# Cross-attention weights of a transformer stack, turned by 32x32 blocks and two transfers instead of transposes on TensorE

## The chip, the cores and the metric

The kernel runs on one core of a Trainium2 chip. The metric is the device time of one execution in microseconds. Before the change it is 2530.57 us, the median of three runs (2528.28 to 2533.17).

The engines are named as in the profile: PE (TensorE, matrix products; PEld is its loading of stationary operands), DVE (VectorE), ACT (ScalarE), POOL (GpSimd) and SP (SyncE, which issues the transfers). PSUM is the memory that PE writes its results to.

## The reference

Four attention blocks follow each other on a tensor x of 8 batches x 256 rows x 128 features, with a context of 8 x 64 rows x 64 features and a mask of 8 x 256 x 256. The third block is a stack of six layers, and the change touches only that one. Each layer does

```
tn = norm(t);  t = mha(tn, tn,  skv, sq, sow, sob, mask)     + t     # self-attention
tn = norm(t);  t = mha(ctx, tn, ckv, cq, cow, cob, ctx_mask) + t     # cross-attention
tn = norm(t);  t = t + (relu(tn @ w1 + b1) @ w2 + b2)
```

with 16 heads of 64, so `ckv` is 64 x 2048 (keys and values), `cq` 128 x 1024 and `cow` 1024 x 128. In `mha` the scores of a head are q k^T / 8, then a softmax, the sum of values, and the product with the output weights.

In cross-attention the keys come from a context that never changes. So for each head the product of query and key weights (64 x 128) and that of value and output weights can be made once a layer and used for all eight batches. This is called folding below.

## The kernel before

All arithmetic is in float32. Activations `t` stay on the chip; weights of a layer are loaded ahead into buffers of which there is one each. Work is written as small steps, each given a tick and a phase with `at(tick, phase, fn)`. At the end (L1195 to L1211) the steps are issued in the order of tick and phase, and each instruction of PE, DVE, ACT and POOL is chained to the one before it on its engine. So the order on these four engines is the written one: an engine that waits holds back everything behind it. SP is not chained; its transfers are put in an order when the program is built.

A layer starts at tick T0. Batch b has its self-attention at T0 + 4b to T0 + 4b + 6 (`plan_sa`, L818), overlapping with its neighbours, cross-attention begins at T_ca = T0 + 32 (`plan_ca`, L1018), and the feed-forward part at T_ca + 16. "Tick 20" below means T0 + 20. In the profiled second layer the scores of tick 20 start on PE at 714.12 us, those of tick 21 at 721.38, 22 at 728.83, 23 at 736.35, 24 at 744.11, 26 at 758.83, 27 at 767.37, 28 at 775.78, 29 at 779.57 and 30 at 789.04.

In a self-attention tick PE does two score tiles (L866), then by turns the values (L921), the output product `out_proj` (L939), and the projections of a later batch: k and q (L829) and v (L848). DVE adds the mask and takes the row minimum of each score quarter (L880), ACT does the exponentials (L885), DVE the reciprocal of the sums (L893), POOL the division (L895), and DVE turns the result by 32x32 blocks (L905, `turn`) for the values. DVE and ACT each empty one of the two tiles of the values ("o copy", L284 and L286), and ACT empties the projections. `add_out` (L945) adds the output product to `t` on DVE in phase 8.2.

PSUM holds four tiles of two banks (`two_banks`, L45), used in turn: a new tile waits until the tile four allocations back is emptied. The "o" buffers on the chip (`big("o")`) are also four in turn; the values of self-attention, the hidden layer of the feed-forward part and the transposed cross-attention weights use them.

The weights of cross-attention are prepared by `plan_ca_weights(l, T)` with T = T_ca - 6, at the end of self-attention. In ticks 26 and 27 `turned` makes eight 128x128 transposes on PE each (L983), of `ckv` (whose keys lie on partitions 0 to 63 and values on 64 to 127) and of `cq`, into one PSUM tile; ACT copies it into an "o" buffer (L989, L991), the queries' one with the scale 1/8. In ticks 28 and 29 `folded` makes AT and WVO with 32 matmuls each (L1001) into two PSUM tiles, which ACT copies (L1007). `keys_both` (L1022) uses AT in tick 30 first.

Each batch's mask is loaded by SP (`load_mask`, L242) into one of two buffers, two ticks ahead of its scores in the written order.

Of the kernel before, what the change touches and what calls it, by code (L numbers as in the profile page):

```python
# [8 lines left out]
F32 = mybir.dt.float32  # L9
# [7 lines left out]
P = 128  # L17
B, S, D = 8, 256, 128
M, DM = 64, 64
NL, H, HD, FF = 6, 16, 64, 512  # L20
HC = H * HD // P
# [6 lines left out]
def tile_xattn_stack(ctx: ExitStack, tc: tile.TileContext, io, out: bass.AP):  # L28
    nc = tc.nc
# [11 lines left out]
    def uniq(base):  # L41
        counter[0] += 1
        return f"{base}_{counter[0]}"

    def two_banks(base):  # L45
        return psum.tile([P, 1024], F32, tag="ps", name=uniq(base))
# [10 lines left out]
    def big(tag, bufs=4, shape=(P, 1024), dtype=F32):  # L57

        return heap.tile(list(shape), dtype, tag=tag, name=uniq(tag), bufs=bufs)

    def sb(shape, tag, bufs=2, pool=None):
        return (pool or act).tile(shape, F32, tag=tag, name=uniq(tag), bufs=bufs)
# [46 lines left out]
    ident = const.tile([P, P], F32, tag="ident", name="ident")  # L109
# [10 lines left out]
    for i in range(4):  # L120
# [52 lines left out]
        out=hmask, in_=hmask, compare_op=ALU.is_ge, fill=0.0, base=0,  # L173
# [3 lines left out]
        out=hmask, in_=hmask, compare_op=ALU.is_ge, fill=0.0, base=7,  # L177
# [3 lines left out]
    for r in range(2):  # L181
        rows = slice(64 * r, 64 * r + 64)
# [10 lines left out]
    W = {}  # L193
# [44 lines left out]
    dram = ctx.enter_context(tc.tile_pool(name="dram", bufs=1, space=bass.MemoryType.DRAM))  # L238
# [40 lines left out]
    def at(tick, phase, fn):  # L279
        plan.setdefault(tick, []).append((phase, fn))  # L280
# [692 lines left out]
    def plan_ca_weights(l, T):  # L973


        st = {}
        W["fold", l] = st

        def turned(name, w, scale):
            def fn():  # L980
                ps = two_banks("tp")
                for c in range(HC):
                    nc.tensor.transpose(  # L983
                        ps[:, c * P : (c + 1) * P], w()[:, c * P : (c + 1) * P], ident
                    )
                st[name] = big("o", shape=(P, HC, P))
                flat = st[name].rearrange("p c x -> p (c x)")
                if scale is None:
                    nc.scalar.copy(flat, ps)  # L989
                else:  # L990
                    nc.scalar.mul(flat, ps, scale)  # L991
            return fn

        def folded(name, cols, w):
            def fn():
                tiles = [two_banks("mm").rearrange("p (c d) -> p c d", c=HC) for _ in range(2)]
                res = sb([P, HC, D], name, 1, heap)
                for c in range(HC):
                    for r in range(2):
                        rows = slice(r * HD, (r + 1) * HD)  # L1000
                        nc.tensor.matmul(  # L1001
                            tiles[r][rows, c, :], lhsT=st["kvT"][rows, c, cols],
                            rhs=w()[rows, c, :], start=True, stop=True,
                        )
                for r in range(2):
                    rows = slice(r * HD, (r + 1) * HD)
                    nc.scalar.copy(res[rows], tiles[r][rows])  # L1007
                st[name] = res
            return fn

        at(T, 3.6, turned("kvT", lambda: W["ca", l][0], None))
        at(T + 1, 3.6, turned("WqT", lambda: W["ca", l][1], HD ** -0.5))
        at(T + 2, 3.6, folded("AT", slice(0, DM), lambda: st["WqT"]))
        at(T + 3, 3.6, folded("WVO", slice(DM, 2 * DM), lambda: W["ca", l][2]))

    keys_of = {}

# [154 lines left out]
    for l in range(NL):  # L1172
        T_ca = T0 + 4 * B
        T_ff = T_ca + 2 * B
        for b in range(B):
            plan_sa(l, b, T0 + 4 * b)
        plan_ca_weights(l, T_ca - 6)
        for b in range(B):
            plan_ca(l, b, T_ca + 2 * b)
            plan_ff(l, b, T_ff + b)  # L1180
        if l > 0:
            at(T0, -1, lambda l=l: load_ff(l))
        if l + 1 < NL:
            at(T_ca + 4, -1, lambda l=l: load_sa(l + 1))
            at(T_ff + 1, -1, lambda l=l: load_ca(l + 1))
        T0 = T_ff + B
# [14 lines left out]
    for tick in sorted(plan):  # L1201
        for _, fn in sorted(plan[tick], key=lambda item: item[0]):
            traced = nc.cur_bb.bb.instructions
            start = len(traced)
# [64 lines left out]
```

## Time and profile before

| what | us | share of the span |
|---|---|---|
| median of the runs | 2530.57 | |
| the profiled execution | 2528.09 | |
| its span, first to last instruction | 2526.4 | |
| PE busy | 2393.0 | 95% |
| DVE busy | 1822.0 | 72% |
| ACT busy | 1735.1 | 69% |
| POOL busy | 1443.0 | 57% |
| sixteen transposes of a layer, busy on PE, six layers (L983) | 13.2 | |
| their two copies on ACT, six layers (L989, L991) | 12.2 | |
| 32x32 turns of 128x512 on DVE, 768 of them (L905) | 519.9, 697 ns each | |
| division on POOL, 128x256, 1,536 of them (L895) | 702.5, 478 ns each | |

The mean granted clock of TensorE is 0.975 of full speed. A line of a timeline has the start in us, the length in us (of all instructions in it when several are merged, x8 for eight), the engine, the line of the kernel, the operation, what it writes and reads, and in brackets how long the engine sat idle before it and what ended that. A line of the chain of work in order of time has start, length, engine, what was written, line and number. Busy times of matmuls overlap each other, so the spacing of starts tells what a group takes of the queue.

### The profile page before, as it was taken

How to read it: one execution, taken by the hardware profiler on the slowest of the kernel's cores; microseconds unless marked ns; L12 is line 12 of the kernel's file. 1: busy time of each engine (PE TensorE's matmuls, PEld its weight loads, DVE VectorE, ACT ScalarE, POOL GpSimd, SP SyncE). 2: the span in 40 equal slices, each digit the busy share in tenths (PEclk: the TensorE clock that was granted, in tenths of full speed). 3: DMA queues.
4: the chain of work that ended last, by engine and by line, in shares of the span. 5: the costliest groups of instructions: out<-in, count | busy, mean ns of one | idle time of the engine just before them, and what ended most of it. 6: DMA issues, size and time to landing. Idle time of an engine off the chain costs nothing.

```text
span 2526.4 us, 100196 instructions
## 1 busy us (share of the span) xinstructions
PE 2393.0 (95%) x42507; PEld 1765.0 (70%) x42507; DVE 1822.0 (72%) x5976; ACT 1735.1 (69%) x4537; POOL 1443.0 (57%) x2477
## 2 busy tenths in 40 slices
PE   6899999999999999999989999989999989999996
PEld 3566777776777776777776777776777776777774
DVE  3677887748887747887747887747887756888764
ACT  3467777657777657777657777657778657778651
POOL 2655556845556844555854555854555763555763
PEclk8999999999999999999999999999999999999996
DMA  5000012000002000002000102000012000000000
GB/s 161 11 2 20 19 35 64 2 8 24 20 28 65 8 7 24 20 20 70 12 2 21 28 20 70 12 2 20 20 28 70 12 2 20 20 20 12 3 1 17
DMA packets 94770, 64.31 MB, mean 25 GB/s; under 512 B 7729, under 2 KB 90353, under 8 KB 94322
## 3 DMA queue, kind: packets, MB, share of 16 engines
q1 hardware_dynamic: 93874, 57.64, 8.3%
q8 instruction: 334, 5.47, 0.9%
q14 instruction: 114, 0.93, 0.1%
q10 hardware_dynamic: 448, 0.26, 0.0%
HBM read 55.78 MB, written 2.10 MB: 23 GB/s over the span
## 4 chain that ended last, share of the span: by engine, by line
PE 69%; POOL 13%; DVE 8%; ACT 7%; issue 3%; DMA 0%; POOLq 0%; DVEq 0%; SPq 0%; ACTq 0%
PE mm L921 14%; PE mm L829 13%; PE sc L866 12%; PE mm L939 7%; PE mm L848 7%; POOL e L360 6%; PE mm L1071 3%; DVE m L359 3%; PE mm L1088 3%; POOL e L372 3%; ACT e L357 2%; PE mm L388 2%; ACT e L885 2%; PE sc L341 1%; POOL rstd L784 1%
## 5 line engine op out<-in xcount | busy, mean ns | idle before, releaser
L895 POOL TENSOR_SCALAR e<-e,rs 128x256 f32<-128x256 f32 x1536 | 702.5, 478 | 690.8 <-DVE rs L893 682.2
L885 ACT ACTIVATE e<-e,mn 128x256 f32<-128x256 f32 x1536 | 758.3, 495 | 131.0 <-DVE mn L880 130.2
L880 DVE CUSTOM_DVE_ANT_0 e<-sc,nm 128x256 f32<-128x256 f32 x1536 | 542.8, 419 | 122.5 <-PE sc L866 122.3
L905 DVE STREAM_TRANSPOSE eTc<-e 128x512 f32<-128x512 f32 x768 | 519.9, 697 | 66.2 <-POOL e L895 64.6
L921 PE MATMUL mm<-eTc,v 32*64 32x256 f32 x12288 | 381.2, 386 | 18.5 <-ACT AT L1007 8.1
L866 PE MATMUL sc<-k,q 64*32 64x256 f32 x12288 | 378.9, 380 | 5.9 <-DVE mn L880 4.2
L921 PEld LDWEIGHTS mm<-eTc,v 32*64 32x64 f32 x12288 | 284.1, 134 | 112.5 <-issue 27.7
L866 PEld LDWEIGHTS sc<-k,q 64*32 64x32 f32 x12288 | 220.2, 106 | 125.3 <-issue 45.8
L360 POOL TENSOR_TENSOR e<-e,m 128x1024 f32<-128x1024 f32 x112 | 213.1, 1903 | 148.6 <-DVE m L359 141.9
L885 ACT ACTIVATION_READ_ACCUMULATOR e<-e,mn 128x1 f32 x1536 | 286.7, 187 | 0.0
L359 DVE TENSOR_REDUCE m<-sc 128x16 f32<-128x1024 f32 x112 | 137.2, 1225 | 179.4 <-ACT e L357 179.4
L388 PE MATMUL mm<-v,k 128*128 128x128 f32 x1792 | 235.5, 287 | 5.9 <-DVE k L380 5.4
L388 PEld LDWEIGHTS mm<-v,k 128*128 128x128 f32 x1792 | 219.1, 200 | 27.4 <-issue 12.1
L341 PE MATMUL sc<-q,tT 128*32 128x256 f32 x3072 | 217.1, 382 | 0.0
L372 POOL TENSOR_TENSOR e<-e,r 128x1024 f32<-128x1024 f32 x112 | 213.2, 1904 | 0.7 <-DVE r L371 0.7
L366 ACT ACTIVATE e<-e 128x1024 f32<-128x1024 f32 x112 | 119.0, 1062 | 115.8 <-POOL e L360 115.8
L829 PE MATMUL mm<-tT,w_sk 128*128 128x256 f32 x768 | 189.6, 390 | 0.0
L286 ACT COPY v<-mm 128x1024 f32<-128x1024 f32 x96 | 97.2, 1012 | 133.1 <-PE mm L848 133.1
L939 PEld LDWEIGHTS mm<-w_sow,o 128*128 128x128 f32 x1536 | 175.1, 192 | 17.7 <-issue 14.4
L848 PE MATMUL mm<-w_sv,tT 128*32 128x256 f32 x3072 | 185.7, 382 | 0.0
L939 PE MATMUL mm<-w_sow,o 128*128 128x128 f32 x1536 | 183.6, 278 | 1.5 <-ACT WVO L1007 1.5
L829 PE MATMUL mm<-tT,w_sq 128*128 128x256 f32 x768 | 173.6, 379 | 0.0
(210 smaller groups left out, 3521.9 us busy)
## 6 DMA issues: line engine op xcount, KB each, us to landing
nm<-mask_d SPq DMA_DIRECT2D x192, 128.0 KB, 3.0
w_sk<-in_L_sa_kv_dram SPq DMA_DIRECT2D x6, 512.0 KB, 9.4
w_sv<-in_L_sa_kv_dram SPq DMA_DIRECT2D x24, 128.0 KB, 2.4
w_sq<-in_L_sa_q_dram SPq DMA_DIRECT2D x6, 512.0 KB, 3.5
w_sow<-in_L_sa_ow_dram SPq DMA_DIRECT2D x6, 512.0 KB, 4.0
w_ckv<-in_L_ca_kv_dram SPq DMA_DIRECT2D x12, 256.0 KB, 4.2
w_cq<-in_L_ca_q_dram SPq DMA_DIRECT2D x6, 512.0 KB, 4.6
w_cow<-in_L_ca_ow_dram SPq DMA_DIRECT2D x6, 512.0 KB, 4.0
```

The source lines that it names most:

```text
L360: nc.gpsimd.tensor_tensor(e, e, m.unsqueeze(2).to_broadcast([P, 16, M]), ALU.subtract)
L372: nc.gpsimd.tensor_tensor(tl["e"], tl["e"], r.unsqueeze(2).to_broadcast([P, 16, M]), ALU.mult)
L388: nc.tensor.matmul(ps[:, :D], lhsT=eT[:, s].rearrange("p q x -> p (q x)"), rhs=vw[:, r, k, g, :], start=(s == 0), stop=(s == 7),)
L829: nc.tensor.matmul(ps[:, i * S : (i + 1) * S], lhsT=w[:, c * P : (c + 1) * P], rhs=st["tT"], start=True, stop=True,)
L848: nc.tensor.matmul(ps[32 * a : 32 * a + 32, i, :], lhsT=st["tT"][:, kb * 32 : (kb + 1) * 32], rhs=sv[:, a].rearrange("p g x -> p (g x)"), ...
L866: nc.tensor.matmul(sc[32 * a : 32 * a + 32, r, j, :], lhsT=st["q"][g][rows, a, qb * 32 : (qb + 1) * 32], rhs=st["k"][g][rows, a, :], start ...
L880: nc.vector.tensor_tensor_reduce(e[:, i, :], sc4[:, i, :], st["nm"][:, 2 * jj + i % 2, :], -1.0, 3.0 * BIG, ALU.add, ALU.min, mn[:, i : i ...
L885: nc.scalar.activation(e[:, i, :], e[:, i, :], AF.Exp, scale=-1.0, bias=mn[:, i : i + 1], accum_out=rs[:, i : i + 1],)
L895: nc.gpsimd.tensor_scalar(e[:, i, :], e[:, i, :], rs[:, i : i + 1], 1.0, ALU.mult, ALU.mult)
L905: nc.vector.transpose(eT[:, r, :, 2 * jj : 2 * jj + 2, :], e[:, 2 * r : 2 * r + 2, :].rearrange("p j (k x) -> p k j x", x=32),)
L921: nc.tensor.matmul(ops[a // 2][r * HD : (r + 1) * HD, a % 2, :S], lhsT=st["v"][kb // 4][rows, kb % 4, (2 * g + r) * HD : (2 * g + r + 1) * ...
L939: nc.tensor.matmul(st["ps"][:, j * D : (j + 1) * D], lhsT=st["oT"][c // 4][:, c % 4, j * P : (j + 1) * P], rhs=sow[:, c, :], start=(c == 0 ...
```

## The change

Both weights are now transposed without PE. `turned(i)`, i = 0 for `ckv` and 1 for `cq`, in ticks 20 and 21 at phase 8.7, turns a whole 128x1024 weight tile by 32x32 blocks in one DVE instruction into an "o" buffer z, and stores z with four transfers of 128 KB into a buffer in device memory. `fetched(i)`, in ticks 22 and 23 at phase -0.5, loads it back with one transfer of 512 KB over the weight tile itself, with the blocks' positions exchanged, so that after it the tile holds the transposed weights in runs of 32 elements. `regrouped`, in tick 27 at phase 8.05, copies the key and value weights on POOL into another order in an "o" buffer, so that 64 columns lie together as the stationary operand of `folded`. The query weights are read by `folded` as they lie, as a moving operand of four runs of 32. The scale 1/8 moves to the copies of AT on ACT. `folded` stays in ticks 28 and 29.

```diff
-        def turned(name, w, scale):
-            def fn():
-                ps = two_banks("tp")
-                for c in range(HC):
-                    nc.tensor.transpose(
-                        ps[:, c * P : (c + 1) * P], w()[:, c * P : (c + 1) * P], ident
-                    )
-                st[name] = big("o", shape=(P, HC, P))
-                flat = st[name].rearrange("p c x -> p (c x)")
-                if scale is None:
-                    nc.scalar.copy(flat, ps)
-                else:
-                    nc.scalar.mul(flat, ps, scale)
-            return fn
-
-        def folded(name, cols, w):
+        def turned(i):
+
+
+            w = W["ca", l][i]
+            z = big("o", shape=(P, 4, HC, 32))
+            nc.vector.transpose(z, w.rearrange("p (c j x) -> p j c x", j=4, x=32))
+            zd = dram.tile([4, 32, 4, HC * 32], F32, tag="wd", name=uniq("wd"), bufs=2)
+            for j in range(4):
+                nc.sync.dma_start(
+                    out=zd[j].rearrange("b i x -> i b x"),
+                    in_=z[:, j].rearrange("p c x -> p (c x)"),
+                )
+            W["cab", l, i] = zd
+
+        def fetched(i):
+            w = W["ca", l][i]
+            nc.sync.dma_start(out=w, in_=W.pop(("cab", l, i)).rearrange("j b i x -> (j b) (i x)"))
+            st[i] = w.rearrange("p (i c x) -> p i c x", i=4, x=32)
+
+        def regrouped():
+
+            st["kvT"] = big("o", shape=(P, HC, 4, 32))
+            nc.gpsimd.tensor_copy(st["kvT"].rearrange("p c i x -> p i c x"), st[0])
+
+        def folded(name, part, w, scale=None):
...
-                            tiles[r][rows, c, :], lhsT=st["kvT"][rows, c, cols],
-                            rhs=w()[rows, c, :], start=True, stop=True,
+                            tiles[r][rows, c, :],
+                            lhsT=st["kvT"][rows, c, 2 * part : 2 * part + 2, :].rearrange(
+                                "p i x -> p (i x)"
+                            ),
+                            rhs=w(c)[rows], start=True, stop=True,
...
-                    nc.scalar.copy(res[rows], tiles[r][rows])
+                    if scale is None:
+                        nc.scalar.copy(res[rows], tiles[r][rows])
+                    else:
+                        nc.scalar.mul(res[rows], tiles[r][rows], scale)
...
-        at(T, 3.6, turned("kvT", lambda: W["ca", l][0], None))
-        at(T + 1, 3.6, turned("WqT", lambda: W["ca", l][1], HD ** -0.5))
-        at(T + 2, 3.6, folded("AT", slice(0, DM), lambda: st["WqT"]))
-        at(T + 3, 3.6, folded("WVO", slice(DM, 2 * DM), lambda: W["ca", l][2]))
+        for i in range(2):
+            at(T - 6 + i, 8.7, lambda i=i: turned(i))
+            at(T - 4 + i, -0.5, lambda i=i: fetched(i))
+        at(T + 1, 8.05, regrouped)
+        at(T + 2, 3.6, folded("AT", 0, lambda c: st[1][:, :, c, :], HD ** -0.5))
+        at(T + 3, 3.6, folded("WVO", 1, lambda c: W["ca", l][2][:, c, :]))
```

## The prediction

> **What bounds the kernel now.** I read the page's busy shares and chain first, then the chain of work in order of time around the touched steps, then each engine's timeline there. Times are those of the second of the six layers; in all six the touched ticks show the same 1.02 us steps and the same DVE and ACT waits, to 0.1 us but for instruction-issue gaps. "Tick n" counts from the layer's T0.
>
> Busy shares, and the shares of the chain by engine:
>
> ```profile
> PE 2393.0 (95%) x42507; PEld 1765.0 (70%) x42507; DVE 1822.0 (72%) x5976; ACT 1735.1 (69%) x4537; POOL 1443.0 (57%) x2477
> PE 69%; POOL 13%; DVE 8%; ACT 7%; issue 3%; DMA 0%; POOLq 0%; DVEq 0%; SPq 0%; ACTq 0%
> ```
>
> TensorE is the bound over most of the span, and DMA is on no part of the chain. The chain through ticks 26 to 28 (start, length, what):
>
> ```profile
> 766.42 1.02 PE tp L983 x8
> 767.44 1.89 PE sc L866 x64
> ...
> 774.83 1.02 PE tp L983 x8
> 775.85 1.11 PE sc L866 x32
> ...
> 781.20 1.85 POOL e L895 x4
> ```
>
> Both removed steps lie on the chain, 1.02 us each. After the scores of tick 28 the chain leaves TensorE for DVE, POOL and ACT. PE's timeline there, idle time in brackets:
>
> ```profile
> 777.67 1.96 PE L1001 MATMUL mm<-o,o 64*64 64x128 f32 x32
> 779.57 1.96 PE L866 MATMUL sc<-k,q 64*32 64x256 f32 x64
> 782.50 0.66 PE L921 MATMUL mm<-eTc,v 32*64 32x256 f32 x8 [0.98 <-ACT AT L1007]
> 783.53 3.68 PE L921 MATMUL mm<-eTc,v 32*64 32x256 f32 x120 [0.37 <-ACT AT L1007]
> ```
>
> So after the AT fold (L1001) PE runs ahead and waits for ACT to empty its two PSUM tiles. DVE's timeline where the new turns go:
>
> ```profile
> 721.40 0.71 DVE L905 STREAM_TRANSPOSE eTc<-e 128x512 f32<-128x512 f32 x1 [0.19 <-POOL e L895]
> 722.58 0.42 DVE L880 CUSTOM_DVE_ANT_0 e<-sc,nm 128x256 f32<-128x256 f32 x1 [0.47 <-PE sc L866]
> ...
> 728.67 0.71 DVE L905 STREAM_TRANSPOSE eTc<-e 128x512 f32<-128x512 f32 x1 [0.20 <-POOL e L895]
> 730.03 0.42 DVE L880 CUSTOM_DVE_ANT_0 e<-sc,nm 128x256 f32<-128x256 f32 x1 [0.66 <-PE sc L866]
> ...
> 745.31 0.42 DVE L880 CUSTOM_DVE_ANT_0 e<-sc,nm 128x256 f32<-128x256 f32 x1 [0.67 <-PE sc L866]
> ```
>
> DVE has about half a microsecond free at the end of ticks 20 and 21, less than one turn. Last, POOL in tick 27 and ACT in tick 28:
>
> ```profile
> 772.79 3.65 POOL L895 TENSOR_SCALAR e<-e,rs 128x256 f32<-128x256 f32 x8 [4.89 <-DVE rs L893]
> ```
>
> ```profile
> 781.47 2.02 ACT L1007 COPY AT<-mm 64x1024 f32<-64x1024 f32 x2
> ```
>
> [...] eight in a row take only 1.02 us of the queue, 128 ns each; I use the spacing. [...] The trace's two 128x512 turns issue in 1.22 us (718.08 to 719.30)[...]. [...] Here POOL's one-input L895 takes 3.65 us for eight of 256, so 1.8 us per 1,024. [...] the 128 KB mask loads here land in 3.0 us.
>
> **The change, part by part.**
>
> *Removed from PE:* 2 steps x 1.02 us x 6 layers = 12.24 us. Is this really recovered? In ticks 26 and 27, DVE stood idle 1.44 and 1.62 us before the next scores, ACT 0.61 and 0.60, POOL 4.89 and 4.76, so all can follow PE 1.02 us earlier per step. The PSUM rotation gets shorter by one tile per tick; the tile that then comes four allocations back is freed in time (add_out ends at 767.14, the values of tick 27 would want it at 768.24; the v copy ends near 767.5). The two ACT copies (1.01 and 1.02 us) go too, worth nothing: ACT waits on both sides of them.
>
> *Added to DVE:* one turn of 128x1024 in each of ticks 20 and 21. Price: 2 x 0.61 = 1.22 us of queue; [...] upper end two rows of 697 ns, 1.39. No row of this size exists, but L905 and L380 read or write equally scattered runs of 32. Behind it in DVE's order is L880, which starts ACT's exponentials, then POOL's division. Tick 20: DVE is free at about 722.04, the turn ends at 723.26, L880 wanted 722.58: 0.68 late. That lateness goes round through ACT and POOL to the last turns of tick 21 (728.67), so the second turn starts near 729.99 and ends near 731.2, against 730.03: 1.17 late. Ticks 22 and 23 have no free time on DVE outside this loop (it is busy 7.65 of 7.76 us in tick 23), so 1.17 stays. Who waits? The values of tick 23 want the PSUM tile that add_out frees: 737.15 + 1.17 = 738.32 against 738.24. The scores of tick 24 want the tile that the o copy frees: 743.21 + 1.17 + 0.04 = 744.42 against 744.11. PE thus loses about 0.3 us per layer ([...] 0.6 with 1.39), and then DVE's idle 0.67 and the following gaps absorb the rest: 6 x 0.3 = 1.8 us.
>
> *Added to POOL:* the copy `regrouped` behind the eight divisions of tick 27. These start 1.02 earlier, at 771.77, and end at 775.42. With 1.8 us the copy ends at 777.22 [...]. But the AT fold, which reads kvT, would like to start at 777.67 - 2.04 = 775.63. So a new wait of about 1.63 us appears on PE, between the scores of tick 28 and the fold. It is nearly free: the fold then ends at 779.2, just before ACT gets to copy it (781.47 - 2.04 = 779.43). The scores of tick 29 end at 781.05, where the values could have begun at 780.46, and of these 0.59 us the 0.37 us second wait takes most: 8 matmuls end at 781.7 against 781.49. PE is about 0.2 late, and the next wait for ACT (0.24 us at 791.61) takes that. So the cost is 0 up to a copy of about 1.87 us, and each microsecond above costs one per layer. A copy of half that price gains nothing more, since ACT's chain then decides. POOL's own next work (781.20 - 2.04 = 779.16) waits for nothing. I take 1.8 us and 0.
>
> *The fold's operands:* the rhs of AT is now four runs of 32 instead of 128 in a row, the weights stay 64 in a row. The trace has no such rhs; L303 reads runs of 128 from a strided tile at 386 ns, like the contiguous L921. I take 0[...]. Scaling on the AT copy instead: 0 (1,015 against 1,002 ns for 128x1024).
>
> *Added to SP:* per layer 8 stores of 128 KB and 2 loads of 512 KB. Stores leave by about 724 and 732, loads by about 728 and 737, landing in 3.5 to 9.4 us as the weight loads do. The first need is POOL's at 775: over 25 us of cover. Behind them in SP's queue are mask loads; in before one is issued at 710.65 and the next near 740.6, wanted at about 745 and 775, so neither is pressed. [...] *The o buffers:* z0 and z1 stand between the oT tiles; the tile four back has passed its out_proj each time (tick 22.3 for the one wanted at 23.3), and z0 is stored long before tick 25. 0.
>
> Sum: -12.24 + 1.8 + 0 = -10.4 us. The profiled span of 2526.4 becomes 2516.0. That execution took 2528.09 us, 1.69 over its span and 2.5 under the median; from the median 2530.57 it makes 2520.2.
>
> **The rivals.** *A, DVE's lateness takes more:* a turn at 1.39 us or beyond, or lateness that reaches the q and k projections. For it: tick 23 is full on DVE. Against: PE's slack there is 0.9 to 1.1 us by the rows above. At 1 us a layer the time is 2524. *B, the wait on kvT decides and the kernel ends slower:* POOL's copy in the place of the removed transposes. After DVE's 0.3 there remain 1.74 us a layer, so it breaks even at a copy of 1.87 + 1.74 = 3.6 us and is slower by 0.2% from 4.5 us, 2.5 times the rate of L895. For it: no plain copy and no access of 32-element runs is on POOL in the trace. Against: L517 and L643, with broadcast operands, still run at 1.76 and 2.04 ns an element. At 5 us: 2530.57 - 12.24 + 1.8 + 6 x 3.1 = 2539. A middle copy of 3 us gives 2527. *C, all of it is gained:* the turns are absorbed entirely: 2518.3. *D, the steps are not recovered because SP's transfers come late:* [...] a store placed behind a long weight-load wait would hold z and kvT. Against: 25 us of cover. At 2 us a layer: 2532.
>
> **How the numbers follow.** C 0.15, the forecast 0.50, A 0.13, a middle B (a copy near 3 us) 0.11, B proper 0.07, D 0.04. No change measurable here is about 0.2%, 5.06 us, so faster begins below 2525.5. Faster: 0.15 + 0.50 + 0.09 of A = 0.74; same: 0.04 of A, 0.10 of B's middle and 0.01 of D = 0.15; slower: 0.07 of B proper, 0.03 of D and 0.01 of the middle B = 0.11. The range runs from C with the runs' scatter of 2 us (2516) to the middle B (2528); the forecast's own is 2518 to 2523.
>
> **What would show it.** L983 gone and the scores of ticks 27 and 28 following the v projection without a gap; L880 of tick 22 about 1.2 us late, and a PE wait of some tenths on DVE in tick 23 or 24; a wait of 1 to 2 us at the AT fold on POOL's copy, with the following wait on ACT AT shrunk from 0.98 towards 0.3; no wait on the DMA loads. The prediction is wrong if the POOL copy exceeds 2 us by much, if the fold with scattered rhs lasts longer than 1.96 us, or if PE waits on DVE beyond tick 24.

## The result, and the profile after

The changed kernel takes 2510.18 us (median of six runs, 2509.0 to 2514.18) against 2529.43 us for the kernel before on the same chip (six runs, 2522.92 to 2533.8). The ratio is 0.9927, with a 95% interval of 0.9911 to 0.9943. It is 19.25 us faster; 10.4 were forecast, and the time lies below the range of 2516 to 2528.

Busy shares, and shares of the chain by engine:

```profile
PE 2379.0 (95%) x42411; PEld 1750.7 (70%) x42411; DVE 1832.8 (73%) x5988; ACT 1721.9 (69%) x4525; POOL 1449.0 (58%) x2483
PE 69%; POOL 13%; ACT 7%; DVE 7%; issue 3%; DMA 0%; POOLq 0%; DVEq 0%; SPq 0%; ACTq 0%
```

PE has lost 96 matmuls (16 x 6) and is as much the bound as before; DMA is still on no part of the chain. The chain through ticks 26 to 28 of the second layer (start, length, what):

```profile
764.31 1.89 PE sc L866 x64
766.19 3.64 PE mm L921 x128
769.83 1.86 PE mm L848 x32
771.70 1.11 PE sc L866 x32
```

Both 1.02 us pieces of L983 are gone, and the scores of tick 28 follow the v projection without a gap (769.83 + 1.86 against 771.70), as do those of tick 27. PE's timeline from the AT fold on, idle time in brackets:

```profile
774.34 1.96 PE L1010 MATMUL mm<-w_cq,o 64*64 64x128 f32 x32 [0.76 <-POOL o L1001]
...
778.36 0.66 PE L921 MATMUL mm<-eTc,v 32*64 32x256 f32 x8 [0.17 <-ACT AT L1022]
779.40 3.68 PE L921 MATMUL mm<-eTc,v 32*64 32x256 f32 x120 [0.38 <-ACT AT L1022]
```

A new wait of 0.76 us on POOL's copy stands ahead of the fold, and the wait for ACT has shrunk from 0.98 to 0.17: the idle time has moved, not grown. The fold over runs of 32 takes the same 1.96 us. The load and the copy of the key and value weights, in ns (shortest/median/longest, then first and last start in us):

```profile
L995 SPq DMA_DIRECT2D w_ckv<-wd x6: 338/341/347, 347.1 to 2255.4; - x6
L1001 POOL COPY o<-w_ckv x6: 1032/1036/1037, 391.2 to 2299.2; 128x1024 f32<-128x1024 f32 x6
```

From the first load's issue (347.1) to the POOL copy (391.2) there are 44 us, and no PE instruction of these ticks waits for a transfer. POOL in tick 27:

```profile
769.65 3.65 POOL L895 TENSOR_SCALAR e<-e,rs 128x256 f32<-128x256 f32 x8 [3.87 <-DVE rs L893]
773.25 1.04 POOL L1001 COPY o<-w_ckv 128x1024 f32<-128x1024 f32 x1
777.04 3.20 POOL L895 TENSOR_SCALAR e<-e,rs 128x256 f32<-128x256 f32 x7 [2.76 <-DVE rs L893]
```

The copy takes 1.04 of the 3.8 us that POOL is idle there. ACT then empties the AT tiles, now with the scale, in 2.05 us (2.02 before).

DVE's timeline in ticks 20 to 23:

```profile
719.23 0.71 DVE L905 STREAM_TRANSPOSE eTc<-e 128x512 f32<-128x512 f32 x1 [0.20 <-POOL e L895]
719.87 1.20 DVE L984 STREAM_TRANSPOSE o<-w_ckv 128x1024 f32<-128x1024 f32 x1
720.99 0.39 DVE L880 CUSTOM_DVE_ANT_0 e<-sc,nm 128x256 f32<-128x256 f32 x1
...
727.68 1.20 DVE L984 STREAM_TRANSPOSE o<-w_cq 128x1024 f32<-128x1024 f32 x1
728.81 0.38 DVE L880 CUSTOM_DVE_ANT_0 e<-sc,nm 128x256 f32<-128x256 f32 x1
```

The idle time that stood ahead of L880 (0.47 and 0.66 us before) is filled. This layer begins 2.18 us earlier than before (its tick 20 at 711.94 instead of 714.12), so these two L880 are 0.59 and 0.96 us late (722.58 and 730.03 before).

**Where the 19 us are.** In the second layer ticks 20 to 30 take 784.91 - 711.94 = 72.97 us instead of 789.04 - 714.12 = 74.92. That is 1.95 us, or 11.7 over six layers. (Summed over all six layers of the two traces it is 11.2, since two layers of before and three of after hold extra gaps of 0.4 to 0.9 us, which the trace puts down to issue or to no wait.) The rest comes in jumps of one or two microseconds, of both signs, in the feed-forward part and at the start of the next layer, where nothing was edited. There the trace shows TensorE's clock at half speed for windows of 3.4 us, now and then two in a row. Before, in the second layer's own approach (stretch and length in us; busy time of PE, PEld, DVE, ACT and POOL; granted clock; DMA share; GB/s):

```profile
508.60:512.00 3.40, 0.73 (x5) 0.35 (x4) 3.21 (x5) 1.48 (x4) 3.07 (x6) 1.00 0.00 0
512.00:515.40 3.40, 3.40 (x16) 3.40 (x17) 2.89 (x9) 1.51 (x2) 3.23 (x4) 0.50 0.00 0
```

The first stretch holds a wait of PE for ACT's normalization, and the next one runs at 0.50. PE's line behind that wait:

```profile
511.54 0.84 PE L809 MATMUL tp<-ident,xn 128*128 128x128 f32 x2 [2.61 <-ACT xn L795]
```

The same place after the change:

```profile
506.90:510.30 3.40, 1.74 (x13) 1.53 (x14) 3.31 (x9) 1.36 (x3) 3.23 (x5) 1.00 0.00 0
510.30:513.70 3.40, 3.40 (x14) 2.95 (x13) 2.94 (x7) 1.03 (x2) 3.07 (x6) 0.50 0.00 0
```

So both kernels have such stretches; the question is how many, and why. Between 400 and 2440 us all twelve half-clock stretches of before, and all nine of after, start on one grid of 3.413 us, to within 1 ns. PE was not idle for the whole of the window ahead: here it was busy 0.73 and 1.74 us of the 3.40.

The runs' own clocks tell the amount. Within runs of one and the same kernel, the time falls by 1.77 us for each 0.001 of mean granted clock (one slope fitted through the 13 sets of runs in this study and the 102 further runs of the kernel before). The size is plausible by an estimate from these numbers: one halved window is 3.41 / 2530 x 0.5 = 0.00067 of mean clock, so 1.2 us by this slope, which is under the 1.7 us that half of its length is. The mean clock is 0.9739 over all runs of before and 0.9778 over the twelve of after. "At equal clock" below means the mean of a set, moved to 0.978 with this slope. It is an adjustment and not a measurement: for two kernels below, whose edits can be read from PE's timeline in every layer, it differs from the timeline by 2 to 3 us.

### The profile page after: what moved, and what is told of

Same layout as the page of the kernel before. It is cut to its first block, busy times and chain, and to the rows that moved or that the text cites. A ratio compares the mean times of both kernels' runs of the same rounds, so it can differ in the third digit from the quotient of the medians.

```text
span 2511.1 us, 100146 instructions
## 1 busy us (share of the span) xinstructions
PE 2379.0 (95%) x42411; PEld 1750.7 (70%) x42411; DVE 1832.8 (73%) x5988; ACT 1721.9 (69%) x4525; POOL 1449.0 (58%) x2483
## 3 DMA queue, kind: packets, MB, share of 16 engines
q1 hardware_dynamic: 101938, 70.22, 10.1%
## 4 chain that ended last, share of the span: by engine, by line
PE 69%; POOL 13%; ACT 7%; DVE 7%; issue 3%; DMA 0%; POOLq 0%; DVEq 0%; SPq 0%; ACTq 0%
PE mm L921 14%; PE mm L829 13%; PE sc L866 12%; PE mm L939 7%; PE mm L848 7%; POOL e L360 6%; PE mm L1088 3%; DVE m L359 3%; PE mm L1105 3%; POOL e L372 3%; ACT e L357 2%; ACT e L885 2%; PE mm L388 2%; PE sc L341 1%; POOL rstd L784 1%
## 5 line engine op out<-in xcount | busy, mean ns | idle before, releaser
L895 POOL TENSOR_SCALAR e<-e,rs 128x256 f32<-128x256 f32 x1536 | 702.5, 478 | 673.8 <-DVE rs L893 665.2
L880 DVE CUSTOM_DVE_ANT_0 e<-sc,nm 128x256 f32<-128x256 f32 x1536 | 542.2, 418 | 100.4 <-PE sc L866 100.2
L388 PE MATMUL mm<-v,k 128*128 128x128 f32 x1792 | 228.5, 281 | 5.5 <-DVE k L380 4.9
L388 PEld LDWEIGHTS mm<-v,k 128*128 128x128 f32 x1792 | 211.6, 194 | 27.3 <-issue 12.0
```

The lines of the kernel that those rows point to most:

```text
L388: nc.tensor.matmul(ps[:, :D], lhsT=eT[:, s].rearrange("p q x -> p (q x)"), rhs=vw[:, r, k, g, :], start=(s == 0), stop=(s == 7),)
L880: nc.vector.tensor_tensor_reduce(e[:, i, :], sc4[:, i, :], st["nm"][:, 2 * jj + i % 2, :], -1.0, 3.0 * BIG, ALU.add, ALU.min, mn[:, i : i ...
L895: nc.gpsimd.tensor_scalar(e[:, i, :], e[:, i, :], rs[:, i : i + 1], 1.0, ALU.mult, ALU.mult)
```

## The experiments

Two theories were set against each other. The texts recorded for the kernels as they are and for the first filling call their first versions L (the rest is how often the clock was halved in the runs that happened to be drawn) and S (something lasting outside the touched ticks); the later ones are P and A. P, for phase: the edit's own ticks give about 12 us, and the rest comes because the length of the layer decides how PE's waits fall into the clock windows. A: the rest comes from what was added or rearranged.

**Both kernels again, unchanged.**

> The kernel before once more, unchanged, for its granted clock in each run and the scatter of medians. Theory L (the change is worth about 12 us in the touched ticks, the rest of the measured 19 us is how often TensorE's clock was halved in the runs that were drawn): the ratio to before is 1.000 within 0.002, single runs scatter over some 10 us, and a run's time falls by about 2.5 us for each 0.001 of granted clock. Theory S (something lasting outside the touched ticks is worth the other 7 us): the same ratio, but clock and time need not go together.

> The changed kernel once more, unchanged. Theory L: the difference of medians moves with the clock that was granted; set to equal clock with the slope of the runs, it is 11 to 14 us. Theory S: again 17 to 21 us, and still so at equal clock.

| runs | number | mean clock | median us | ratio (95%) | us at equal clock |
|---|---|---|---|---|---|
| r_before | 14 | 0.9737 | 2530.59 | 1.0004 (0.9995 to 1.0013) | 2522.6 |
| r_after | 6 | 0.9773 | 2510.95 | 0.9925 (0.9909 to 0.9941) | 2509.7 |

The difference holds, and so does the clock's. At equal clock all runs of before stand at 2522.8 and the two sets of after at 2511.3 and 2509.7: 12.3 us apart. The clock's difference of 0.0039 is worth 6.9 us. Together 19.2. In time the gap is the 17 to 21 us of S, at equal clock the 11 to 14 of L: the clock's difference is itself lasting, which neither had said. The slope is 1.77 us for each 0.001, not the 2.5 expected.

**The added parts and the removed parts at once.** On top of the changed kernel, the sixteen transposes and two copies are made again, with results that nothing reads.

```diff
+        def unused(i):
+            ps = two_banks("tp")
+            for c in range(HC):
+                nc.tensor.transpose(
+                    ps[:, c * P : (c + 1) * P], W["ca", l][i][:, c * P : (c + 1) * P], ident
+                )
+            nc.scalar.copy(big("o", shape=(P, HC * P)), ps)
+
+        at(T, 3.6, lambda: unused(0))
+        at(T + 1, 3.6, lambda: unused(1))
```

> The changed kernel with the sixteen transposes and two copies of before put back in their old ticks, their results unused: all that the change adds, nothing that it removes. Runs so far show a time of 2527.8 us for before and 2514 to 2517 for after at a granted clock of 0.975, 1.8 us for each 0.001 of clock, and a mean clock of 0.974 for before and 0.978 for after. Theory P (the number of halved clock windows of 3.41 us follows from how the layer's length stands to them): the layer is as long as before again, so the clock is 0.974 and the time 2528 to 2534. Theory A (something that the change adds, or its other order of transfers and buffers, keeps the clock up): clock 0.978, time 2521 to 2525.

2529.44 us, ratio 0.9994 (0.9987 to 1.0002), mean clock 0.9740, 2522.4 at equal clock. With the layer's length back, the clock is back as well, and the whole gain is gone: turns, stores, loads, the POOL copy and the scattered operand together cost nothing that shows in the time, and bring nothing. From tick 20 to tick 30 the second layer takes 75.02 us against 74.92 before, so they cost about 0.1 us a layer there. That speaks for P and against A. PE's timeline:

```profile
777.50 1.09 PE L1029 MATMUL tp<-ident,w_cq 128*128 128x128 f32 x8
...
780.41 1.96 PE L1010 MATMUL mm<-w_cq,o 64*64 64x128 f32 x32
...
785.25 0.66 PE L921 MATMUL mm<-eTc,v 32*64 32x256 f32 x8 [0.99 <-ACT AT L1022]
```

With PE's own 1.02 us back, the fold waits for POOL no longer and the wait for ACT is 0.99 again, as before the change (0.98).

**The removal alone.** The kernel before without transposes and copies. It leaves out the transposition: the folds read the weights as they were loaded, so what it computes is not the attention of the reference.

```diff
-        at(T, 3.6, turned("kvT", lambda: W["ca", l][0], None))
-        at(T + 1, 3.6, turned("WqT", lambda: W["ca", l][1], HD ** -0.5))
+        def as_loaded():
+            st["kvT"] = W["ca", l][0].rearrange("p (c x) -> p c x", c=HC)
+            st["WqT"] = W["ca", l][1].rearrange("p (c x) -> p c x", c=HC)
+
+        at(T + 1, 3.6, as_loaded)
```

> The kernel before with the transposes and their copies left out and nothing in their place: the folds read the weights as they were loaded, so the attention weights are not transposed. All that the change removes, nothing that it adds. Theory P: 12.2 us less at equal clock, and nearly the layer length of after, so a clock near 0.978: 2508 to 2512. Theory A: the same 12.2 us at the clock of before: 2515 to 2518.

2507.01 us, ratio 0.9909 (0.9896 to 0.9921), mean clock 0.9788, 2508.7 at equal clock. The removal brings the clock of after without any of the added work, and the time is a little below the 2508 to 2512 that P expected. Ticks 20 to 30 of the second layer take 72.88 us, 2.04 less than before, which makes the chain's 12.2 over six layers. At equal clock it is 14.1 us, so 1.9 of that lie outside these ticks or are an error of the adjustment.

**More work in the kernel before.** If length decides, then lengthening must be able to raise the clock too. Six unused matmuls (twelve records, 1.44 us of PE's queue) ahead of the first transposes of each layer:

```diff
                 ps = two_banks("tp")
+                for _ in range(6 if name == "kvT" else 0):
+                    nc.tensor.matmul(ps[:, :P], lhsT=ident, rhs=ident, start=True, stop=True)
                 for c in range(HC):
```

> The kernel before with six unused 128x128 matmuls (1.4 us of TensorE's queue, by the 0.23 us that one took in the filled kernel) ahead of the first transposes of each layer. It makes the layer as much longer than before as brings it to the length of after plus one window of 3.41 us. Theory P: the clock rises to about 0.978, and of 6 x 1.4 = 8.5 us only some 2 are left: 2529 to 2533. Theory A: the clock stays at 0.974 and all of it is paid: 2536 to 2539.

2527.42 us, ratio 0.9985 (0.9979 to 0.9992), mean clock 0.9785, 2528.1 at equal clock. More work on the bounding engine made the kernel a little faster than before, and than the 2529 to 2533 that P expected. Ticks 20 to 30 take 76.31 us in each layer against 74.92, so the work itself costs 1.39 us a layer or 8.3 in all (5.3 at equal clock), and more than that is won elsewhere. In its trace seven halved windows are left in the layers, of fourteen in the trace of before; those at the feed-forward part are gone but for one. The place where before had its first halved window, on this kernel's clock grid:

```profile
511.50:514.90 3.40, 1.47 (x14) 1.27 (x12) 2.71 (x6) 1.74 (x3) 3.07 (x6) 1.00 0.00 0
514.90:518.30 3.40, 2.66 (x20) 2.42 (x21) 2.89 (x10) 2.28 (x4) 3.40 (x3) 1.00 0.00 0
```

PE's wait for ACT is as long as before (2.62 us against 2.61), but it now falls into two windows, which leaves PE busy 1.47 us of the first instead of 0.73, and the clock stays at 1.00. P stands: no account without the clock has this sign. It also answers a third theory, that the transposes as such keep the clock down, since all sixteen are still in this kernel.

**Filling PE's waits, first attempt.** If the halved windows follow PE's waits for the normalization in the feed-forward part, unused matmuls in these waits should remove them.

```diff
-    def ahead(b, stats_at, normal_at, tT_at, g, bias, st, on_scalar=True):
+    def ahead(b, stats_at, normal_at, tT_at, g, bias, st, on_scalar=True, fill=0):
...
         def trans():
-            ps = tp_tile()
+            ps = two_banks("tp")
+            for _ in range(fill):
+                nc.tensor.matmul(ps[:, 512:640], lhsT=ident, rhs=ident, start=True, stop=True)
             xn = st.pop("xn")
...
-        ahead(b, (T - 3, 6), (T - 2, 3.3), (T - 1, 2.9), pre_g[:, l : l + 1], pre_b[:, l : l + 1], st)
+        ahead(b, (T - 3, 6), (T - 2, 3.3), (T - 1, 2.9), pre_g[:, l : l + 1], pre_b[:, l : l + 1], st,
+              fill=(16, 11, 0, 0, 0, 0, 0, 0)[b])
```

> The kernel before with unused 128x128 matmuls, 16 and 11 of them per layer, put on TensorE in the two longest waits of a layer (2.6 and 1.9 us, before the transposes of the feed-forward part's batches 0 and 1). Their results are not used and nothing is left out. Theory L: the halved windows that follow the 2.6 us wait go (one of 3.4 us in most layers, worth up to 1.7 us each), the mean clock rises to about 0.982, and the time falls by 4 to 10 us. Theory S has no reason for any gain: no change or slower by up to a few us.

> The changed kernel with the same unused matmuls. Theory L: it falls by 3 to 10 us too, and its distance to the filled kernel before is 11 to 14 us, since a part of what varied with the clock is taken away from both. Theory S: the distance stays at 17 to 21 us.

The same edit in both kernels gave 2536.72 us, ratio 1.0032 (1.0021 to 1.0042), clock 0.9795, from before, and 2520.38 us, ratio 0.9965 (0.9951 to 0.9979), clock 0.9825, from after. Both are slower than without it, where L expected 3 to 10 us less. It was sized and placed wrongly: the waits stand ahead of batches 1 and 2, not 0 and 1, and each of these 128x128 float32 matmuls takes two records and 0.24 us, as this row of the filled before shows for the 16 of them:

```profile
507.32 3.84 PE L808 MATMUL tp<-ident 128*128 128x128 f32 x32
```

3.84 us of work went where PE did not wait. At equal clock the filling costs 17 us from before and 18 from after (2540.0 and 2528.5), and yet the clock rose by 0.0056 and 0.0047.

**The same, placed right.** The filling is 9 and 6 matmuls ahead of batches 1 and 2; the edit is otherwise the one above.

```diff
+              fill=(0, 9, 6, 0, 0, 0, 0, 0)[b])
```

> The changed kernel with unused matmuls in the two longest waits of a layer, now ahead of the right transposes (batches 1 and 2 of the feed-forward part) and short enough for the waits (9 and 6, about 2.1 and 1.4 us in 2.6 and 1.9). Nothing is left out. Both theories: no cost in a layer; the windows halved by these waits go, the clock rises to 0.981 or more, and the time falls by 4 to 9 us, to 2502 to 2507. If the waits are not what halves the clock, the time stays at 2511 or rises.

> The kernel before with the unused matmuls in the same two waits as in the filled kernel after that ran at 2504.8 us. If the change is worth 12 us in the touched ticks and the other 6 to 7 us are halved clock windows behind these waits, both filled kernels have a clock near 0.980 and stand 11 to 14 us apart: 2516 to 2519. If the change has a lasting gain elsewhere, they stand 18 us apart: 2522 to 2525.

From after: 2504.78 us, ratio 0.9897 (0.9884 to 0.991), clock 0.9810, 2509.7 at equal clock. It beats both kernels by doing work that nothing needs. From before: 2514.89 us, ratio 0.9931 (0.9919 to 0.9944), clock 0.9828, 2523.0 at equal clock. Here the filling is free at equal clock, and 15.6 us come from the clock alone; the time is a little below the 2516 to 2519 expected. PE in the filled after:

```profile
507.16 2.17 PE L808 MATMUL tp<-ident 128*128 128x128 f32 x18
509.94 0.71 PE L811 MATMUL tp<-ident,xn 128*128 128x128 f32 x2 [0.61 <-ACT xn L795]
...
515.22 1.60 PE L808 MATMUL tp<-ident 128*128 128x128 f32 x12
517.22 0.71 PE L811 MATMUL tp<-ident,xn 128*128 128x128 f32 x2 [0.39 <-ACT xn L795]
```

The waits of 2.62 and 1.93 us at this place in after have become 0.61 and 0.39. The stretches on its clock grid, columns as above:

```profile
508.70:512.10 3.40, 2.73 (x22) 2.33 (x21) 3.13 (x9) 1.72 (x3) 3.23 (x5) 1.00 0.00 0
512.10:515.50 3.40, 3.40 (x46) 2.38 (x46) 3.09 (x7) 1.86 (x6) 3.07 (x6) 1.00 0.00 0
```

PE is busy for 2.73 us of the first, and the second keeps the full clock. In the layers of this trace six halved windows are left, all at the start of a layer, and none in the feed-forward part. The two filled kernels differ by 13.3 us at equal clock, the edit's own gain once more; in time they differ by 10.1, under the 11 to 14 expected, since their clocks differ (0.9828 and 0.9810).

**The POOL copy.** Made three times over, to test the prediction's break-even at 3.6 us and its slack of 1.87 us.

```diff
-            nc.gpsimd.tensor_copy(st["kvT"].rearrange("p c i x -> p i c x"), st[0])
+            for _ in range(3):
+                nc.gpsimd.tensor_copy(st["kvT"].rearrange("p c i x -> p i c x"), st[0])
```

> The changed kernel with its POOL copy of the key and value weights made three times over (about 3.1 us instead of 1.04). The prediction's reading: PE's wait at the AT fold grows from 0.76 to about 2.8 us, and what is over the slack towards ACT (a copy of about 1.7 to 1.9 us in all) is paid one to one: 7 to 9 us slower than the changed kernel at equal clock, so about 2523 to 2525 set to a clock of 0.975. Rivals: every microsecond of the wait is paid, 12.4 us; or none, since POOL is idle there, 0 to 1 us.

2536.0 us, ratio 1.0023 (1.0015 to 1.0031), clock 0.9686, 2519.3 at equal clock. There it lies 8 to 9.6 us above the two sets of after, which is what the slack asks for, with 3.25 us for the three copies in the trace: 6 x (3.25 - 1.87) = 8.3. In time it lies 26 us above. The trace shows why:

```profile
782.45 3.40 PE L1011 MATMUL mm<-w_cq,o 64*64 64x128 f32 x32 [2.97 <-POOL o L1002]
...
787.66 4.01 PE L921 MATMUL mm<-eTc,v 32*64 32x256 f32 x128
```

The fold now waits 2.97 us, no wait for ACT is left behind it, and the fold itself takes 3.40 us instead of 1.96. The clock in the two stretches:

```profile
778.60:782.00 3.40, 0.88 (x35) 0.33 (x16) 3.27 (x17) 2.82 (x12) 3.28 (x5) 1.00 0.56 159
782.00:785.40 3.40, 2.95 (x28) 2.95 (x30) 2.92 (x10) 1.29 (x6) 2.85 (x7) 0.50 0.48 120
```

A halved window follows this wait in five of the six layers. PE was busy 0.88 us of the stretch that holds most of the wait, and the wait cost more than its length here: to its 2.97 us come the 1.44 us by which the fold lasts longer behind it.

**The POOL copy one tick earlier.**

```diff
-        at(T + 1, 8.05, regrouped)
+        at(T, 8.05, regrouped)
```

> The changed kernel with the POOL copy one tick earlier (tick 26). The prediction's reading: PE's wait of 0.76 us at the AT fold is gone, and the next wait, on ACT's copy of AT, grows from 0.17 back to about 0.9 us, so the time at equal clock is the same within 1.5 us. Rival: the wait was a loss, 4.6 us faster.

2510.64 us, ratio 0.9921 (0.9908 to 0.9935), clock 0.9774, 2510.7 at equal clock: the same as after. PE's timeline:

```profile
771.85 2.40 PE L1010 MATMUL mm<-w_cq,o 64*64 64x128 f32 x32
...
776.69 0.66 PE L921 MATMUL mm<-eTc,v 32*64 32x256 f32 x8 [0.55 <-ACT AT L1022]
```

The fold no longer waits for POOL, and the wait for ACT has grown to 0.55. In this layer the fold itself takes 2.40 us instead of 1.96, and the trace names no wait for the 0.44 more; in three of the six layers it takes 1.96 and the wait for ACT is 0.99 to 1.00, as before the change. The 0.76 us wait of the changed kernel was therefore free: ACT decides behind it.

**The DVE turns.** Each made twice.

```diff
-            nc.vector.transpose(z, w.rearrange("p (c j x) -> p j c x", j=4, x=32))
+            for _ in range(2):
+                nc.vector.transpose(z, w.rearrange("p (c j x) -> p j c x", j=4, x=32))
```

> The changed kernel with each of its two DVE turns made twice, 2.4 us instead of 1.2 in ticks 20 and 21. The prediction's reading: DVE's lateness in tick 22 grows from about 1.0 to more than 3 us, PE's slack of 0.9 to 1.1 us in ticks 23 and 24 is used up, and PE loses about 2 us a layer more: 10 to 14 us slower than the changed kernel at equal clock, which takes away the gain. Rival: DVE's idle time takes it, 0 to 3 us.

2537.1 us, ratio 1.0025 (1.0018 to 1.0032), clock 0.9740, 2529.9 at equal clock: 19 to 20 us more than after, where 10 to 14 were expected. PE in tick 23:

```profile
738.15 5.40 PE L921 MATMUL mm<-eTc,v 32*64 32x256 f32 x128 [2.36 <-DVE t L946]
```

The wait is on `add_out` (L946), as the prediction had it for a longer turn, and six such waits make 14.2 us. A halved window follows in each of the six layers. So the mechanism is shown, and one turn more per tick leaves DVE's slack far behind. The products behind the wait take 5.40 us instead of the 3.71 of after, at a halved clock; with the wait that is 4.05 us a layer, or 24.3 of the 26.9 us by which the kernel is slower in time. Each halved window thus costs 1.69 us here, where the slope takes off 1.2. That explains about 3 of the 5 us that stand beyond the waits at equal clock; the rest stays open.

## Why the prediction was wrong in size

**Removed, -12.24: right.** The price was taken from the spacing of starts, 128 ns a transpose (1.02 us for eight), where the trace of before has 279 ns as the mean busy time of one. The two pieces are gone from the chain, DVE's first L880 of ticks 27 and 28 start 0.95 and 1.98 us earlier against tick 20 (765.44 and 772.83 instead of 768.57 and 776.99), and the removal alone shortens its own ticks by 2.04 us a layer.

**DVE, +1.8: right in mechanism, too high.** The turn took 1.20 us (1.22 priced), and L880 came 0.59 and 0.96 us late (0.68 and 1.17 worked out). On PE this left 0.05 to 0.07 us a layer at the scores of tick 24 (742.00 - 711.94 = 30.06 instead of 744.11 - 714.12 = 29.99) where 0.3 was priced, so 0.4 us in all. The PE wait of some tenths on DVE in tick 23 or 24, which the prediction named as a sign, is not in the trace. The doubled turn shows that this was a real edge.

**POOL, 0: right, on a price that was too high.** The copy took 1.04 us instead of the 1.8 that follow from the rate of L895. The wait at the fold was 0.76 instead of 1.63. The copy made three times agrees with the slack of 1.87 at equal clock; rival B's break-even at 3.6 us does not hold for the time, since at 3.25 us the kernel is already slower than before, through the clock.

**Operands, SP, o buffers, the scale, 0: right.** With the transposes back, the kernel with all additions is within 0.4 us of before at equal clock, and within 0.1 us a layer in its own ticks. Rivals A and D did not occur.

**The step that failed** is the last one of the sum: "The profiled span of 2526.4 becomes 2516.0." It lets everything outside the touched ticks run as before, and the range adds only "the runs' scatter of 2 us". The sum lacked a term for the mean granted clock, which went from 0.9739 to 0.9778 and is worth 6.9 us. The miss of 10.0 us (2520.2 against 2510.2) is made up of this 6.9, of 1.9 by which the gain at equal clock was larger (12.3 instead of 10.4), and of 1.1 by which the runs of before beside the result lie under the median that the prediction started from (2529.43 against 2530.57), up to rounding. Of the 1.9, most is DVE's 0.4 in the place of 1.8: the touched ticks of the second layer gave 11.7. How the gain splits between the ticks and the clock is known to 2 or 3 us only, by the errors of the adjustment named above. The page's clock of 0.975 was in sight, and so was PE's wait of 2.6 us for L795 in the trace of before; what was not asked is whether such a wait slows what follows it. The sign of this term could not have been told from the edit alone: six matmuls more in the same place raised the clock as well. That it came out as a gain here is luck. It belonged into the range.

One reservation: the two profiled executions differ by only 0.0012 in clock, with fourteen and thirteen halved windows in the layers (fourteen and twelve in those of the unchanged kernels run again), and by 15.15 us in time, which is 13.0 at equal clock. Both profiled executions of after (2512.94 and 2514.54 us) are among the longer ones of their sets. The larger difference of clock rests on the runs' records, not on this pair of traces.

## What to carry to other kernels

Before adding up an edit on a kernel that TensorE bounds, look where the granted clock is below 1 and which wait stands in the window ahead; an edit that only shifts the work can add or remove halved windows elsewhere (here six matmuls more a layer left seven of fourteen), so the sum needs a term for the clock of both signs. Compare kernels at equal clock as well as by their times, or a few tenths of a per cent will be credited to the wrong part; and read the edit's own ticks beside it, since the adjustment was off by 2 to 3 us here. Filling PE's waits of 2.6 and 1.9 us with unused matmuls cut to their length won 5 us on one kernel here and 15 on the other.

## What the runs showed of the hardware

- In before and after, between 400 and 2440 us, the clock was halved in windows of 3.413 us, on one grid in each trace, one or two in a row. In these two traces the full-clock window ahead of a halved one had PE busy between 0.22 and 0.59 of its length, by the start and end of the matmul records, and one ahead of another at full clock 0.48 or more. So between 0.48 and 0.59 both occur, and the traces do not show what decides. In the stretches printed above it is 0.26 ahead of a halved one in x_pool3, and 0.43 (pad6_before) and 0.80 (fill2_after) ahead of one at full clock. In before and after, halved windows that were followed by a second one had PE busy 0.92 of their length, those that ended the halving 0.86 to 1.00.
- PE waits of 0.84 and 0.90 us close together, at the start of a layer, stood in the window from 578.6 us of after (PE busy 0.49 of it), and two halved ones followed.
- The mean clocks of the kernels here lie between 0.969 and 0.983. By the slope of 1.77 us for each 0.001 that is an estimated 25 us on a kernel of 2.5 ms.
- A POOL copy of 128x1024 in runs of 32 elements took 1.04 us, and a PE product whose moving operand lies in four runs of 32 took 1.96 us for 32 matmuls of 128 columns, as one with 128 in a row.
